# Norm offsets on GpSimd, layer 2's divide on ScalarE, and new booked durations in a planned four-layer graph network

## Chip, cores and metric

The kernel runs on one core of a Trainium2 chip. The metric is the device time in microseconds (us). Engines are named as the profile names them: PE (TensorE, matmul), PEld (its weight loads), DVE (VectorE), ACT (ScalarE), POOL (GpSimd), SP (SyncE, which issues nearly all DMAs).

## The reference

`x` is 32 batches of 512 nodes with 128 features, `adj` a 512x512 weighted adjacency. Four layers follow one another, each as `x = x + layer(relu(layernorm(x)))`:

```
def _layernorm(x, axis=-1, eps=1e-5):
    m = jnp.mean(x, axis=axis, keepdims=True)
    v = jnp.var(x, axis=axis, keepdims=True)
    return (x - m) / jnp.sqrt(v + eps)

# layer 0, GCN:   out = (d (adj+I) d) h W^T + b
# layer 1, GGNN, 5 steps of:
    m_in = adj @ h ; m_out = adj @ h ; av = [m_in, m_out]
    z  = sigmoid(av @ w3.T + u3(h)) ; r = sigmoid(av @ w4.T + u3(h))
    hv = tanh(av @ w5.T + u5(r * h)) ; h = (1 - z) * h + z * hv
# layers 2 and 3, graph attention, h = x W:
    e = leaky_relu(h a_src [i] + h a_dst [j]), masked by adj
    out = softmax(e) @ h          # layer 2: elu(out)
```

All inputs and outputs are fp32.

## The kernel before, in words

A batch is a tile of 128 partitions x 4 chunks x 128 features, 128x512 in the profile. Each batch passes through `gcn` (layer 0, two batches at a time), `ggnn` (layer 1, five calls of `step`) and `gat` twice (layers 2 and 3). Many batches are in flight at once: six "lanes" of layer 1, nine `x` buffers, eight PSUM banks.

**The order of the work.** Nothing is emitted as it is written. Each piece is booked with `op(engine, cost, due, emit, r, w)`: the engine, a cost in us, a due time, a function that issues the instructions, and the values read and written. A `Plan` then simulates all engines with these costs, a delay for the handover from each engine to another (`DELAY`, L64), and the buffers that are free. It tries several ways of setting the priorities (8 rounds for each of two `ends`, each round taking its due times from a pass backwards over the last one), keeps the order with the earliest simulated end, and emits the instructions of every engine's queue in that order. The queues are in order on the chip: an instruction that waits holds up all behind it. So booked costs are not only a description: they decide the order, in all engines' queues and in SP's queue of DMAs. Booked names: `MM` a fp32 matmul of 512 columns, `MR` one in fp32r, `V` a 128x512 operation of DVE, `A` a 128x512 activation, `COPY` a 128x512 copy or scaling by ACT.

**Products in three parts.** A product in layers 0 and 1 (`in_three`, L626) splits its operand into `upper`, `lower` and `across` (`operands`, L612: one ACT instruction, L615, and two of DVE, L616 and L618). PE multiplies `upper` and `lower` (L642), ACT rescales the bank in place (`rescale`, L624), and PE adds `across`. `step` does the same with the gates (L756) and has plain fp32 products (L753). Its gates are ACT's tanh (L786, L793, L797) and DVE's arithmetic (L788, L799, L800, L802).

**The norm.** `norm_relu` (L516) is called by `gcn`, `ggnn` and by `gat` for all but the last four batches: 119 times, and once as `norm_first`. DVE takes statistics of each chunk (L507), aggregates (L511) and adds epsilon (`ve`, L512). POOL raises this to -0.5 (`rstd`, L520). DVE multiplies the mean by -1 and by `rstd` (`off`, L523). ACT applies `relu(rstd * x + off)` in four instructions (L526). For batches 1 to 3 a DVE multiply by `dinv` (L522) follows the power. The last four batches (`near`) use another norm, `center_relu`.

**The turn of tokens to features** is a DVE transpose of 32x32 blocks (`sq`, L592 and L602) and DMAs by way of DRAM, on SP's queue (L595, L597, L605, L608), or PE transposes in the first and last batches.

**Attention.** `gat` (L848): PE makes heads (L869), ACT takes exponents (L885) and scales (L889), a small DMA pair spreads a row over all partitions (L907, L909), DVE makes the weights `e` (L912), and PE mixes (L938) two chunks at a time into a bank, with the softmax's denominator in column `D`. DVE takes its reciprocal `rden` (L941). For layer 2 DVE then divides both chunks in one instruction from the bank, `v = bank * rden` (L943); ACT takes an exponent of `v` (L962), and two DVE instructions (L964, L966) finish the ELU and the residual. Layer 3 divides and adds in one (L948).

Of the kernel before, what the change touches and what calls it, by code (L numbers as in the profile page):

```python
# [10 lines left out]
F32 = mybir.dt.float32  # L11
# [3 lines left out]
ALU = mybir.AluOpType  # L15

P = 128
EPS = 1e-5
# [41 lines left out]
class Plan:  # L60

    DELAY = {"PE": 0.24, "ACT": 0.15, "DVE": 0.12, "POOL": 0.1, "SP": 2.4, "AQ": 2.4}  # L64

    IDLE = 0.11
    SPAN, REST = 3.4, 0.9
# [203 lines left out]
def gnn_stack(ctx: ExitStack, tc: tile.TileContext, a: dict, out: bass.AP):  # L271
    nc = tc.nc
    x, adj = a["x"], a["adj"]
    B, N, D = x.shape
# [46 lines left out]
        IDLE_FROM, lambda v: nc.tensor.transpose(v.t[:, 0, :], ident.t, ident.t))  # L321
    op = plan.op
    MM, MM1, TURN, MR = 0.858, 0.224, 0.111, 0.2325
    V, A, COPY = 0.595, 0.575, 0.495

    def fixed(shape, name, parts=1, dtype=F32):
        v = Val(None, parts)
        v.t = tiles(1, shape, name, dtype=dtype)[0]
        return v
# [13 lines left out]
        return flat(v.t) if len(v.t.shape) == 3 else v.t  # L343

    ident = fixed([P, P], "ident")
    mhalf = fixed(SMALL, "mhalf")
    warm = Val("hv")
    op("POOL", 0.8, -1000, lambda: make_identity(nc, ident.t), w=[ident])
    op("POOL", 0.1, -999, lambda: nc.gpsimd.memset(mhalf.t, -0.5), w=[mhalf])
    op("DVE", 0.1, -1000, lambda: nc.vector.memset(warm.t[:, 0, :], 0.0), w=[warm])  # L350
    op("ACT", 1.4, -1000, lambda: nc.scalar.activation(warm.t[:, 1, :1], warm.t[:, 0, :1], AF.Tanh), r=[warm])

# [149 lines left out]


    def norm_stats(b, due):
        xb, st, mv, ve = xs[b], Val("st", C), Val("mv"), Val("ve")
        for c in range(C):
            op("DVE", 0.192, due, lambda c=c: nc.vector.bn_stats(st.t[:, c, :], xb.t[:, c, :]), r=[xb[c]], w=[st[c]])  # L507

        def aggr():
            for c in range(C):  # L510
                nc.vector.bn_aggr(mv.t[:, c, :], st.t[:, c, :])  # L511
            nc.vector.tensor_scalar_add(ve.t, mv.t[:, :, 1], EPS)  # L512
        op("DVE", 0.33, due, aggr, r=[st], w=[mv, ve])
        return mv, ve

    def norm_relu(b, y, due, times=None):  # L516

        xb, off, rstd = xs[b], Val("off"), Val("rstd")
        mv, ve = norm_stats(b, due)
        op("POOL", 1.0, due, lambda: nc.gpsimd.tensor_tensor(rstd.t, ve.t, mhalf.t, ALU.pow), r=[ve, mhalf], w=[rstd])  # L520
        if times:
            op("DVE", 0.1, due, lambda: nc.vector.tensor_mul(rstd.t, rstd.t, times.t), r=[times], w=[rstd])  # L522
        op("DVE", 0.1, due, lambda: nc.vector.scalar_tensor_tensor(off.t, mv.t[:, :, 0], -1.0, rstd.t, op0=ALU.mult, op1=ALU.mult),  # L523
           r=[mv, rstd], w=[off])
        for c in range(C):
            op("ACT", 0.385, due, lambda c=c: nc.scalar.activation(  # L526
                chunk(y, c), xb.t[:, c, :], AF.Relu, bias=off.t[:, c:c + 1], scale=rstd.t[:, c:c + 1]),
               r=[xb[c], off, rstd], w=[y[c * len(y.writers) // C]])

    def norm_first(b, y):  # L530

        xb, off, f = xs[b], Val("off", C), Val("rstd", C)
        mv, ve = norm_stats(b, -802)
        for parts in ((0, 2, 1), (3,)):
            some = slice(min(parts), max(parts) + 1)
            fs, offs = [f[c] for c in parts], [off[c] for c in parts]

            def power(c=parts[-1], some=some):
                nc.vector.reduce_sum(deg.t[:, c:c + 1], adj_sb.t[:, c, :], axis=mybir.AxisListType.X)
                nc.vector.scalar_tensor_tensor(f.t[:, some], deg.t[:, some], 1.0, ve.t[:, some], op0=ALU.add, op1=ALU.mult)  # L540
            op("DVE", 0.8, -801.5, power, r=[ve, adj_sb[parts[-1]], *(deg[c] for c in parts[:-1])], w=[*fs, deg[parts[-1]]])
            op("POOL", 1.0, -802, lambda some=some: nc.gpsimd.tensor_tensor(
                f.t[:, some], f.t[:, some], mhalf.t[:, some], ALU.pow), r=[mhalf], w=fs)
            op("DVE", 0.1, -801.5, lambda some=some: nc.vector.scalar_tensor_tensor(
                off.t[:, some], mv.t[:, some, 0], -1.0, f.t[:, some], op0=ALU.mult, op1=ALU.mult), r=[mv, *fs], w=offs)
        op("DVE", 0.2, -800.5, lambda: nc.vector.tensor_scalar(
            y.t[:, 0, :], xb.t[:, 0, :], mv.t[:, 0, 0:1], 0.0, op0=ALU.subtract, op1=ALU.max), r=[xb[0], mv], w=[y[0]])
        op("DVE", 0.2, -802, lambda: nc.vector.tensor_scalar_mul(y.t[:, 0, :], y.t[:, 0, :], f.t[:, 0:1]), r=[f[0]], w=[y[0]])
        for c in range(1, C):
            op("ACT", 0.385, -798, lambda c=c: nc.scalar.activation(  # L550
                y.t[:, c, :], xb.t[:, c, :], AF.Relu, bias=off.t[:, c:c + 1], scale=f.t[:, c:c + 1]), r=[xb[c], off[c], f[c]], w=[y[c]])
        op("DVE", 0.1, -801, lambda: nc.vector.tensor_scalar_add(dinv.t, deg.t, 1.0), r=[deg], w=[dinv])
        op("POOL", 1.0, -801, lambda: nc.gpsimd.tensor_tensor(dinv.t, dinv.t, mhalf.t, ALU.pow), r=[mhalf], w=[dinv])
# [34 lines left out]
    def shuttle(src, squares, dst, due, soon):  # L588


        sq, far = Val("sq"), Val("far", Q)
        op("DVE", 0.617, soon, lambda: nc.vector.transpose(  # L592
            sq.t.rearrange("p q (c j) -> p q c j", c=C), flat(src.t).rearrange(squares, c=C, q=Q)), r=[src], w=[sq])
        for k in range(Q):
            op("SP", 0.44, due, lambda k=k: nc.sync.dma_start(  # L595
                far.t[:, :, k, :].rearrange("q i f -> i q f"), sq.t[k * W:(k + 1) * W]), r=[sq], w=[far[k]], delay=4)
        op("SP", 0.4, due, lambda: nc.sync.dma_start(dst.t, far.t.rearrange("q i k f -> (q i) k f")), r=[far], w=[dst], delay=5)  # L597

    def shuttle_first(h, hT, due, soon):

        sq, far = Val("sq"), Val("far", Q)
        op("DVE", 0.617, soon, lambda: nc.vector.transpose(  # L602
            sq.t.rearrange("p k (c i) -> p k c i", c=C), h.t.rearrange("p c (k j) -> p k c j", k=Q)), r=[h], w=[sq])
        for q in range(Q):
            op("SP", 0.44, due, lambda q=q: nc.sync.dma_start(  # L605
                far.t[:, :, q, :].rearrange("k j f -> j k f"), sq.t[q * W:(q + 1) * W]), r=[sq], w=[far[q]], delay=4)
        for q in range(Q):
            op("SP", 0.4, due, lambda q=q: nc.sync.dma_start(  # L608
                hT.t.rearrange("p c (q i) -> q p c i", q=Q)[q], far.t.rearrange("k j q (c i) -> q (k j) c i", c=C)[q]),
               r=[far[q]], w=[hT[q]], delay=5)  # L610

    def operands(src, given, made, due):  # L612

        upper, lower, across = Val("upper"), Val("lower"), Val("across")
        op("ACT", COPY, due - 5, lambda: nc.scalar.mul(made(upper.t), given(src.t), BELOW), r=[src], w=[upper])  # L615
        op("DVE", 0.575, due - 5, lambda: nc.vector.tensor_sub(made(lower.t), given(src.t), made(upper.t).bitcast(F32)),  # L616
           r=[src, upper], w=[lower])
        op("DVE", 0.575, due - 5, lambda: nc.vector.scalar_tensor_tensor(  # L618
            flat(across.t), flat(lower.t).bitcast(F32), -SPLIT, flat(upper.t).bitcast(F32), op0=ALU.mult, op1=ALU.add),
           r=[lower, upper], w=[across])  # L620
        return upper, lower, across
# [226 lines left out]
    def gat(b, l, due):  # L848
# [60 lines left out]
            op("SP", 0.4, due + 1.5, lambda: nc.sync.dma_start(  # L909
                row.t, line.t.rearrange("c q i -> (c q i)").unsqueeze(0).to_broadcast([P, N])), r=[line], w=[row, e], delay=7)  # L910
        for j in range(C):
            op("DVE", 0.65, due + 3, lambda j=j: nc.vector.scalar_tensor_tensor(  # L912
                e.t[:, j, :], matrix(row), h.t[:, j, D + 1:D + 2], mask.t[:, j, :], op0=ALU.max, op1=ALU.mult),
               r=[row, h[2 + j // 2], mask], w=[e[j]])

# [14 lines left out]
        for a, p in enumerate(ps):  # L930
# [8 lines left out]
                                         start=(j == 0), stop=(j == C - 1))  # L939
                op("PE", C * MM1, due + 4, mix, r=[e, h], w=[*ps] if a == c == 0 else [p])  # L940
            op("DVE", 0.08, due + 4, lambda some=some, pt=pt: nc.vector.reciprocal(rden.t[:, some], pt()[:, :per, D]), r=[p], w=[rden[c] for c in chunks])  # L941
            if l == 2:
                op("DVE", 0.335, due + 4, lambda some=some, pt=pt: nc.vector.tensor_mul(  # L943
                    v.t[:, some], pt()[:, :, :D], rden.t[:, some, None].to_broadcast([P, 2, D])), r=[p, rden[2 * a], rden[2 * a + 1]], w=[v[a]])
            else:
                def finish(chunks=chunks, pt=pt):
                    for c, i in enumerate(chunks):
                        nc.vector.scalar_tensor_tensor(xb.t[:, i, :], pt()[:, c, :D], rden.t[:, i:i + 1], xb.t[:, i, :],  # L948
                                                       op0=ALU.mult, op1=ALU.add)
                op("DVE", per * 0.26, due + 4, finish, r=[p, *(rden[c] for c in chunks)], w=[xb[c] for c in chunks])  # L950
# [77 lines left out]
```

## Time and profile before

| what | value |
|---|---|
| median of 3 runs | 1538.93 us (1538.82 to 1539.08) |
| the profiled execution | 1538.23 us, its span 1536.4 us |
| granted TensorE clock | 1.00 |
| busy: PE, PEld | 1514.7 us (99%), 1149.8 (75%) |
| busy: DVE | 1475.1 us (96%), 3725 instructions |
| busy: ACT | 1203.0 us (78%), 2608 instructions |
| busy: POOL | 153.7 us (10%), 137 instructions |
| DMA | 157.76 MB, 103 GB/s, queue share 39.9% of 16 engines |

Busy time is the union of an engine's instructions, as a share of the span from the first instruction to the last. Ends of matmuls are modelled in this profile, so a busy PE need not be PE at its peak. Times inside the span count from its start.

### The profile page before, as it was taken

How to read it: one execution, taken by the hardware profiler on the slowest of the kernel's cores; microseconds unless marked ns; L12 is line 12 of the kernel's file. 1: busy time of each engine (PE TensorE's matmuls, PEld its weight loads, DVE VectorE, ACT ScalarE, POOL GpSimd, SP SyncE). 2: the span in 40 equal slices, each digit the busy share in tenths (PEclk: the TensorE clock that was granted, in tenths of full speed). 3: DMA queues.
4: the chain of work that ended last, by engine and by line, in shares of the span. 5: the costliest groups of instructions: out<-in, count | busy, mean ns of one | idle time of the engine just before them, and what ended most of it. 6: DMA issues, size and time to landing. Idle time of an engine off the chain costs nothing.

```text
span 1536.4 us, 24733 instructions
## 1 busy us (share of the span) xinstructions
PE 1514.7 (99%) x7373; PEld 1149.8 (75%) x7373; DVE 1475.1 (96%) x3725; ACT 1203.0 (78%) x2608; POOL 153.7 (10%) x137
## 2 busy tenths in 40 slices
PE   9999999999999999999999999999999999999998
PEld 7666677777777777777777677777777777777778
DVE  8999989999999999999999999999999999998898
ACT  7877788787978687987788868788887788767664
POOL 2101001010001000101110101100011010001011
PEclk9999999999999999999999999999999999999999
DMA  4233244454544444434444435354443544333111
GB/s 110 42 92 101 75 104 104 102 131 112 131 110 117 115 101 118 121 95 129 114 105 117 111 95 139 96 134 111 114 114 87 130 109 114 96 109 84 42 35 43
DMA packets 270150, 157.76 MB, mean 103 GB/s; under 512 B 81248, under 2 KB 236224, under 8 KB 270016
## 3 DMA queue, kind: packets, MB, share of 16 engines
q1 hardware_dynamic: 269728, 155.66, 39.9%
q8 instruction: 58, 0.95, 0.3%
q14 instruction: 76, 0.62, 0.1%
q10 hardware_dynamic: 288, 0.52, 0.1%
HBM read 86.25 MB, written 69.84 MB: 102 GB/s over the span
## 4 chain that ended last, share of the span: by engine, by line
PE 56%; DVE 29%; ACT 6%; issue 4%; DMA 3%; SPq 1%; POOL 1%; DVEq 0%; POOLq 0%; ACTq 0%
PE bank L642 19%; PE bank L753 13%; PE bank L756 11%; PE bank L938 7%; DVE e L912 4%; DVE lower L616 4%; DVE across L618 3%; DVE sq L592 2%; DVE st L507 2%; PE bank L869 2%; ACT bank L624 2%; DVE hv L799 2%; DVE hT L802 1%; ACT y L526 1%; DVE rh L788 1%
## 5 line engine op out<-in xcount | busy, mean ns | idle before, releaser
L624 ACT ACTIVATE bank<-bank 128x512 f32<-128x512 f32 x748 | 426.3, 593 | 117.1 <-PE bank L642 63.3
L520 POOL TENSOR_TENSOR rstd<-ve,mhalf 128x4 f32<-128x4 f32 x119 | 142.1, 1194 | 1303.2 <-DVE ve L512 868.4
L938 PEld LDWEIGHTS bank<-h_gat,e 128*128 128x128 f32 x1792 | 217.8, 191 | 21.5 <-issue 14.1
L618 DVE SCALAR_TENSOR_TENSOR across<-lower,upper 128x512 fp32r<-128x512 f32 x328 | 221.3, 681 | 2.1 <-PE bank L756 0.4
L938 PE MATMUL bank<-h_gat,e 128*128 128x129 f32 x1792 | 220.3, 275 | 0.1
L756 PE MATMUL bank<-upper,gates 128*128 128x512 f32 x420 | 203.9, 486 | 4.4 <-DVE lower L616 2.0
L756 PE MATMUL bank<-across,gates 128*128 128x512 f32 x420 | 202.3, 491 | 2.6 <-ACT bank L624 2.3
L642 PE MATMUL bank<-adj,across 128*128 128x512 f32 x640 | 189.8, 420 | 0.9 <-ACT bank L624 0.7
L642 PE MATMUL bank<-adj,upper 128*128 128x512 f32 x640 | 189.0, 417 | 0.6 <-ACT h_gat L889 0.4
L642 PE MATMUL bank<-adj,lower 128*128 128x512 f32 x640 | 173.3, 393 | 0.0
L756 PE MATMUL bank<-lower,gates 128*128 128x512 f32 x420 | 166.4, 396 | 0.7 <-DVE lower L616 0.7
L753 PE MATMUL bank<-rh,wT 128*128 128x512 f32 x320 | 164.3, 595 | 2.6 <-DVE rh L788 2.4
L753 PE MATMUL bank<-hT,wT 128*128 128x512 f32 x320 | 163.3, 592 | 0.0
L912 DVE SCALAR_TENSOR_TENSOR e<-row,h_gat,maskT 128x512 f32<-128x512 f32 x224 | 156.4, 745 | 0.0
L642 PEld LDWEIGHTS bank<-adj,upper 128*128 128x128 f32 x640 | 117.9, 188 | 41.7 <-issue 14.1
L642 PEld LDWEIGHTS bank<-adj,across 128*128 128x128 f32 x640 | 117.0, 188 | 42.9 <-issue 13.2
L786 ACT ACTIVATE r<-bank,gate_bw 128x512 f32<-128x512 f32 x160 | 111.1, 694 | 40.4 <-PE bank L753 39.2
L642 PEld LDWEIGHTS bank<-adj,lower 128*128 128x128 f32 x640 | 120.2, 188 | 27.1 <-DVE lower L616 0.2
L793 ACT ACTIVATE z<-bank,gate_bw 128x512 f32<-128x512 f32 x160 | 110.4, 694 | 29.0 <-PE bank L756 22.2
L526 ACT ACTIVATE y<-x,off,rstd 128x128 f32<-128x128 f32 x252 | 111.7, 495 | 19.0 <-DVE off L523 18.9
L797 ACT ACTIVATE hv<-bank,gate_bw 128x512 f32<-128x512 f32 x160 | 111.4, 698 | 12.0 <-PE bank L753 11.8
L799 DVE TENSOR_TENSOR hv<-hv,hT 128x512 f32<-128x512 f32 x160 | 108.7, 680 | 11.6 <-ACT hv L797 11.6
(159 smaller groups left out, 2671.0 us busy)
## 6 DMA issues: line engine op xcount, KB each, us to landing
far<-sq SPq DMA_DIRECT2D x928, 64.0 KB
h<-far SPq DMA_DIRECT2D x148, 256.0 KB
gT<-far SPq DMA_DIRECT2D x56, 256.0 KB
row<-line SPq DMA_DIRECT2D x56, 256.0 KB
hT<-far SPq DMA_DIRECT2D x112, 64.0 KB
x<-in_x_dram SPq DMA_DIRECT2D x24, 256.0 KB
out_dram<-x SPq DMA_DIRECT2D x20, 256.0 KB
adjT<-in_x_dram SPq DMA_DIRECT2D x8, 256.0 KB
```

The lines of the kernel that those rows point to most:

```text
L520: op("POOL", 1.0, due, lambda: nc.gpsimd.tensor_tensor(rstd.t, ve.t, mhalf.t, ALU.pow), r=[ve, mhalf], w=[rstd])
L526: op("ACT", 0.385, due, lambda c=c: nc.scalar.activation(chunk(y, c), xb.t[:, c, :], AF.Relu, bias=off.t[:, c:c + 1], scale=rstd.t[:, c:c ...
L618: op("DVE", 0.575, due - 5, lambda: nc.vector.scalar_tensor_tensor(flat(across.t), flat(lower.t).bitcast(F32), -SPLIT, flat(upper.t).bitca ...
L624: op("ACT", COPY, due, lambda: nc.scalar.mul(flat(p.t), flat(p.t), by), w=[p])
L642: nc.tensor.matmul(flat(p.t), left.t[:, c, :], right.t[:, c, :], start=first and c == 0, stop=c == C - 1, skip_group_check=True)
L753: nc.tensor.matmul(flat(p.t), (of or gates).t[:, i, :], flat(moving.t), start=start, stop=True, skip_group_check=True)
L756: nc.tensor.matmul(flat(p.t), of.t[:, i - 1, :], flat(moving.t), start=start, stop=True, skip_group_check=True)
L786: op("ACT", A, due - 5, lambda: nc.scalar.activation(flat(r.t), flat(gate.t), AF.Tanh, bias=gate_b["w4"].t, scale=0.5), r=[gate, gate_b["w ...
L797: op("ACT", A, due - 5, lambda: nc.scalar.activation(flat(hv.t), flat(cand.t), AF.Tanh, bias=gate_b["w5"].t), r=[cand, z, gate_b["w5"]], w ...
L799: op("DVE", V, due - 5, lambda: nc.vector.tensor_sub(flat(hv.t), flat(hv.t), flat(hT.t)), r=[hT], w=[hv])
L912: op("DVE", 0.65, due + 3, lambda j=j: nc.vector.scalar_tensor_tensor(e.t[:, j, :], matrix(row), h.t[:, j, D + 1:D + 2], mask.t[:, j, :], ...
L938: nc.tensor.matmul(pt()[:, c, :D + 1], e.t[:, j, i * P:(i + 1) * P], h.t[:, j, :D + 1], start=(j == 0), stop=(j == C - 1))
```

## The change

Three things change. In the norm, POOL takes over the addition of epsilon and both multiplications of the offset, in three instructions beside its power; two small DVE instructions go (in `norm_first` the addition stays on DVE). In layer 2 of all but the last four batches, the division of the mix is done by ACT, one instruction for each chunk with `rden` as its column of scales, in place of one DVE instruction for two chunks. And booked costs and delays are changed; these issue nothing, but the planned order follows from them. `...` marks unchanged lines.

```diff
-    DELAY = {"PE": 0.24, "ACT": 0.15, "DVE": 0.12, "POOL": 0.1, "SP": 2.4, "AQ": 2.4}
+    DELAY = {"PE": 0.2, "ACT": 0.15, "DVE": 0.145, "POOL": 0.1, "SP": 2.4, "AQ": 2.4}
...
-    V, A, COPY = 0.595, 0.575, 0.495
+    V, A, COPY = 0.6, 0.575, 0.505
...
-    mhalf = fixed(SMALL, "mhalf")
+    mhalf, eps, minus1 = fixed(SMALL, "mhalf"), fixed(SMALL, "eps"), fixed(SMALL, "minus1")
...
-    op("POOL", 0.1, -999, lambda: nc.gpsimd.memset(mhalf.t, -0.5), w=[mhalf])
+    for v, to in ((mhalf, -0.5), (eps, EPS), (minus1, -1.0)):
+        op("POOL", 0.1, -999, lambda v=v, to=to: nc.gpsimd.memset(v.t, to), w=[v])
...
     def norm_stats(b, due):
-        xb, st, mv, ve = xs[b], Val("st", C), Val("mv"), Val("ve")
+        xb, st, mv = xs[b], Val("st", C), Val("mv")
         for c in range(C):
-            op("DVE", 0.192, due, lambda c=c: nc.vector.bn_stats(st.t[:, c, :], xb.t[:, c, :]), r=[xb[c]], w=[st[c]])
+            op("DVE", 0.196, due, lambda c=c: nc.vector.bn_stats(st.t[:, c, :], xb.t[:, c, :]), r=[xb[c]], w=[st[c]])
 
         def aggr():
             for c in range(C):
                 nc.vector.bn_aggr(mv.t[:, c, :], st.t[:, c, :])
-            nc.vector.tensor_scalar_add(ve.t, mv.t[:, :, 1], EPS)
-        op("DVE", 0.33, due, aggr, r=[st], w=[mv, ve])
-        return mv, ve
+        op("DVE", 0.29, due, aggr, r=[st], w=[mv])
+        return mv
 
     def norm_relu(b, y, due, times=None):
 
         xb, off, rstd = xs[b], Val("off"), Val("rstd")
-        mv, ve = norm_stats(b, due)
-        op("POOL", 1.0, due, lambda: nc.gpsimd.tensor_tensor(rstd.t, ve.t, mhalf.t, ALU.pow), r=[ve, mhalf], w=[rstd])
+        mv = norm_stats(b, due)
+        op("POOL", 1.2, due, lambda: nc.gpsimd.tensor_tensor(rstd.t, mv.t[:, :, 1], eps.t, ALU.add), r=[mv, eps], w=[rstd])
+        op("POOL", 1.2, due, lambda: nc.gpsimd.tensor_tensor(rstd.t, rstd.t, mhalf.t, ALU.pow), r=[mhalf], w=[rstd])
+        op("POOL", 1.2, due, lambda: nc.gpsimd.tensor_tensor(off.t, mv.t[:, :, 0], minus1.t, ALU.mult), r=[mv, minus1], w=[off])
         if times:
             op("DVE", 0.1, due, lambda: nc.vector.tensor_mul(rstd.t, rstd.t, times.t), r=[times], w=[rstd])
-        op("DVE", 0.1, due, lambda: nc.vector.scalar_tensor_tensor(off.t, mv.t[:, :, 0], -1.0, rstd.t, op0=ALU.mult, op1=ALU.mult),
-           r=[mv, rstd], w=[off])
+        op("POOL", 1.2, due, lambda: nc.gpsimd.tensor_tensor(off.t, off.t, rstd.t, ALU.mult), r=[rstd], w=[off])
...
# transposes of shuttle and shuttle_first: 0.617 -> 0.626
# lower and across of operands (L616, L618): 0.575 -> V
# e of gat (L912): 0.65 -> 0.661
...
-            if l == 2:
+            if l == 2 and not near:
+                def divide(chunks=chunks, pt=pt):
+                    for c, i in enumerate(chunks):
+                        nc.scalar.mul(v.t[:, i, :], pt()[:, c, :D], rden.t[:, i:i + 1])
+                op("ACT", 0.52, due + 4, divide, r=[p, *(rden[c] for c in chunks)], w=[v[a]])
+            elif l == 2:
                 op("DVE", 0.335, due + 4, lambda some=some, pt=pt: nc.vector.tensor_mul(
                     v.t[:, some], pt()[:, :, :D], rden.t[:, some, None].to_broadcast([P, 2, D])), r=[p, rden[2 * a], rden[2 * a + 1]], w=[v[a]])
```

More of the change, by code (lines that the diff above doesn't have):

```diff
@@ L532, in norm_first @@
         xb, off, f = xs[b], Val("off", C), Val("rstd", C)
-        mv, ve = norm_stats(b, -802)
+        mv, ve = norm_stats(b, -802), Val("ve")
+        op("DVE", 0.1, -802, lambda: nc.vector.tensor_scalar_add(ve.t, mv.t[:, :, 1], EPS), r=[mv], w=[ve])
         for parts in ((0, 2, 1), (3,)):
@@ L591, in shuttle @@
         sq, far = Val("sq"), Val("far", Q)
-        op("DVE", 0.617, soon, lambda: nc.vector.transpose(
+        op("DVE", 0.626, soon, lambda: nc.vector.transpose(
             sq.t.rearrange("p q (c j) -> p q c j", c=C), flat(src.t).rearrange(squares, c=C, q=Q)), r=[src], w=[sq])
@@ L601, in shuttle_first @@
         sq, far = Val("sq"), Val("far", Q)
-        op("DVE", 0.617, soon, lambda: nc.vector.transpose(
+        op("DVE", 0.626, soon, lambda: nc.vector.transpose(
             sq.t.rearrange("p k (c i) -> p k c i", c=C), h.t.rearrange("p c (k j) -> p k c j", k=Q)), r=[h], w=[sq])
@@ L615, in operands @@
         op("ACT", COPY, due - 5, lambda: nc.scalar.mul(made(upper.t), given(src.t), BELOW), r=[src], w=[upper])
-        op("DVE", 0.575, due - 5, lambda: nc.vector.tensor_sub(made(lower.t), given(src.t), made(upper.t).bitcast(F32)),
+        op("DVE", V, due - 5, lambda: nc.vector.tensor_sub(made(lower.t), given(src.t), made(upper.t).bitcast(F32)),
            r=[src, upper], w=[lower])
-        op("DVE", 0.575, due - 5, lambda: nc.vector.scalar_tensor_tensor(
+        op("DVE", V, due - 5, lambda: nc.vector.scalar_tensor_tensor(
             flat(across.t), flat(lower.t).bitcast(F32), -SPLIT, flat(upper.t).bitcast(F32), op0=ALU.mult, op1=ALU.add),
@@ L911, in gat @@
         for j in range(C):
-            op("DVE", 0.65, due + 3, lambda j=j: nc.vector.scalar_tensor_tensor(
+            op("DVE", 0.661, due + 3, lambda j=j: nc.vector.scalar_tensor_tensor(
                 e.t[:, j, :], matrix(row), h.t[:, j, D + 1:D + 2], mask.t[:, j, :], op0=ALU.max, op1=ALU.mult),
```

## The prediction

> **What bounds the kernel now.** I read the page's busy shares first: PE 99%, DVE 96%, ACT 78%, POOL 10%. Two engines look full, so I asked for the busy time in stretches, then for the groups by form, the waits, and short pieces of the timeline. The stretches (columns: us, then busy us and instructions of PE, PEld, DVE, ACT, POOL):
>
> ```profile
> 160.00:280.00 120.00, 119.90 (x498) 87.14 (x497) 108.85 (x229) 98.77 (x199) 7.72 (x6) 1.00 0.38 96
> 280.00:1320.00 1040.00, 1028.04 (x5023) 787.62 (x5022) 1025.70 (x2526) 837.10 (x1811) 99.83 (x85) 1.00 0.45 114
> 1320.00:1480.00 160.00, 160.00 (x784) 117.45 (x783) 142.34 (x340) 115.36 (x258) 11.84 (x10) 1.00 0.29 77
> ```
>
> In the middle 1040 us, when all four layers are in flight at once, DVE is busy 98.6%; on either side of it 89 to 91%. PE's busy share cannot be compared so directly, because matmul ends are modelled. I therefore count slots, the spacing at which matmuls follow one another when nothing holds them. The longest pieces of the chain give it: L642 x12 in 2.77 us is 0.231 us, L753 x8 in 3.43 is 0.429, L938 x24 in 2.68 is 0.112. With the counts of each stretch PE's slots fill 118.9 of 120 us (99.1%), 1011.7 of 1040 (97.3%) and 159.1 of 160 (99.4%). So where DVE has a tenth of its time free PE is the bound and nearly perfect; where DVE is full, PE loses 28 us. **In the middle DVE is the limit, with PE 28 us behind it.**
>
> The groups that the change touches (busy, mean ns of one | idle before, releaser):
>
> ```profile
> L943 DVE TENSOR_TENSOR v<-bank,rden 128x256 f32<-128x256 f32 x64 | 25.2, 415 | 0.1
> L512 DVE TENSOR_SCALAR ve<-mv 128x4 f32<-128x4 f32 x120 | 20.4, 170 | 4.1
> L523 DVE SCALAR_TENSOR_TENSOR off<-mv,rstd 128x4 f32<-128x4 f32 x119 | 18.2, 154 | 8.3 <-POOL rstd L520 7.2
> L889 ACT ACTIVATE h_gat<-bank,h_gat 128x128 f32<-128x128 f32 x224 | 69.8, 388 | 0.9
> L520 POOL TENSOR_TENSOR rstd<-ve,mhalf 128x4 f32<-128x4 f32 x119 | 142.1, 1194 | 1303.2 <-DVE ve L512 868.4
> ```
>
> A mean is not what an instruction takes of its engine, since the next one starts before it ends. The timeline of DVE shows the slot (start, duration):
>
> ```profile
> 708.57 0.17 DVE L512 TENSOR_SCALAR ve<-mv 128x4 f32<-128x4 f32 x1
> 708.65 0.69 DVE L799 TENSOR_TENSOR hv<-hv,hT 128x512 f32<-128x512 f32 x1
> 709.25 0.68 DVE L788 SCALAR_TENSOR_TENSOR rh<-r,hT 128x512 f32<-128x512 f32 x1
> 709.86 0.68 DVE L800 SCALAR_TENSOR_TENSOR hv<-z,hv 128x512 f32<-128x512 f32 x1
> 710.46 0.15 DVE L523 SCALAR_TENSOR_TENSOR off<-mv,rstd 128x4 f32<-128x4 f32 x1
> 710.53 0.28 DVE L507 BATCH_NORM_STATS2 st<-x 128x6 f32<-128x128 f32 x1
> ```
>
> `ve` takes 0.08 us, `off` 0.07, a 512-wide operation 0.60. Two L943 stand in the timeline as one entry of 0.74 us, and the next instruction starts 0.65 after it: 0.325 each. Last, who waits for whom (total us, times, longest):
>
> ```profile
> PEld bank L756 <- ACT bank L624: 27.6, 63, 1.5
> ACT r L962 <- DVE v L943: 27.3, 19, 3.6
> ACT y L526 <- DVE off L523: 24.6, 35, 2.2
> PEld bank L756 <- DVE lower L616: 10.2, 18, 1.7
> PEld bank L753 <- DVE rh L788: 7.1, 12, 1.1
> ```
>
> PE is held by ACT's rescale of a bank (L624) and by DVE's operands; ACT in turn is held by the two kinds of DVE work that the change takes away.
>
> **The Trainium skill.** "Trainium Kernel Development and Optimization", section Performance Expectations, calls matmul busy time a bad measure of closeness to the roofline; here 99% busy stands against 97.3% of slots. "Perfetto Trace Analysis", section Optimizing Scalar/DVE Operations, says that work may be handed from a saturated DVE to ScalarE or even GpSimd, but that GpSimd and DVE share an SBUF read port. The trace shows DVE undisturbed: L799, L788 and L800 above ran at 0.68 to 0.69 us while L520 ran from 708.88 to 710.20; their groups' means are 0.68. "GPSIMD Engine Reference", section 3.1, has an add of 2048 elements at 4497 ns and about 2.6 cycles an element; at 1.2 GHz that leaves some 60 ns, so an estimate for 128x4 is 0.1 us. No row here shows a plain add or multiply on POOL.
>
> **The change part by part.**
>
> 1. *Norm, DVE side.* `ve` leaves 119 norms (`norm_first` keeps one): 119 x 0.08 = 9.5 us. `off` leaves 119: 119 x 0.07 = 8.3 us, with the 7.2 us that DVE stood waiting for POOL's power. In the middle there are 85 of each: 85 x 0.15 = 12.8 us of slots.
>
> 2. *Norm, POOL side.* One power becomes add, power, multiply by -1, multiply. The power is 1.01 to 1.52 us (1.19 mean). The new ones lie between the estimated 0.1 and the power's 1.5; the order books 1.2 for each. I take 0.5, as a dispatch-dominated guess between both ends. Even at 1.3 a norm is 5.2 us, 119 make 620 us of 1536, so POOL is no bound. Its queue issues no DMA. What changes is latency: from aggregate to ReLU 0.08 + 1.19 + 0.07 and two handovers become 2.5 to 5 us on POOL, without DVE's queue in between. Behind it stand ACT's four L526, then their shuttle on SP or the transpose on PE. The order has six batches in flight, and it places L526 by the booked 4 x 1.2, so short operations only leave slack. Cost taken: nothing while they stay within 1.3; the upper end is rival 3. In batches 1 to 3 a DVE multiply by `dinv` lies in the chain; PE is short of work there (37.57 busy of the first 40 us), so up to 2 us may be lost. I take 1.
>
> 3. *Layer 2's divide.* 56 L943 (8 of 64 belong to the last batches and stay) leave DVE: 56 x 0.325 = 18.2 us, in the middle 46 x 0.325 = 15.0. ACT gains 112 multiplies 128x128 from a bank with a column scale, the same form as L889: 69.8 / 224 = 0.31 each, 35 us, taking ACT from 1203 to 1238 us (81%). The wait of L962 for `v` (27.3 us) becomes a wait of the divide for `rden`, behind the same DVE queue; queued behind it on ACT are rescales that PE needs. ACT is 80% busy in the middle (837 of 1040), so I price this at 4 us of PE time, between 0 and 10.
>
> 4. *Durations.* The order is worked out from booked costs before the kernel starts and then frozen into in-order queues. The old book had L616 and L618 at 0.575 where the timeline shows 0.60: 656 x 0.025 = 16.4 us of DVE work that the old order did not know; some 830 other 512-wide ones at 0.595 (4 us), L912 at 0.65 against 0.661 (2.8), transposes (2). Together 25 us, 1.7% of DVE: the order thinks operands ready before they are, and PE waits on L616 and L788. PE's handover is set from 0.24 to 0.20; at 437.66 the matmul after an L753 starts, and the L797 that waited starts at 437.86, so 0.20 is right. This costs no instruction. But it reshuffles everything, SP's queue of shuttles too; the DMAs stay the same in number, and I price them at nothing, since DMA engines are at 45% and a new order shifts them either way.
>
> *The sum.* DVE in the middle: 12.8 + 15.0 of slots and about 3 of waits, 31 us of 1040, so it could end at 1009. PE stays at 1011.7 of slots, and at the 99.2% of the looser stretches needs 1020: at most 20 us come back. DVE would then still be 98% full, so I take 16, less 4 for ACT. Outside the middle PE is at 99% already; 3 us from better order where DVE holds it in 40 to 160, less 1 in the start. 16 - 4 + 3 - 1 = 14 us. The profiled execution took 1538.23 us (span 1536.4 and 1.8 around it), so 1524; the median of the runs is 0.7 higher: **1525 us**.
>
> **Rivals.** (1) *DVE off the bound altogether*: the order, knowing true costs, keeps PE at 99.2% throughout, and the start and tail gain too: 20 in the middle and 5 to 9 elsewhere, 1511. For it: the flanks do this today. Against: ACT fuller. (2) *Gain eaten by ACT*: PE's largest real wait is already ACT (27.6 against 10.2 and 7.1 for DVE); if the 35 us added there return as PE waits one for two, 17 us go and 1536 to 1538 remains. (3) *POOL's chain late in ACT's queue*: where four POOL instructions take more than the booked 1.2 us with its handover, say 1.5 (the power reached 1.52), each norm's L526 comes 4 x 0.2 = 0.8 us late, 119 x 0.8 = 95 us of ACT waiting at its head, of which a quarter reaches PE by the rescales: 24 us against the 14, so 1549, slower. It decides from about 1.43 us for each POOL instruction. For it: L526 already waits 24.6 us. Against: only the power is known to be long. (4) *The order is just another one*: its parameters (ends, slot, idle point) stay, and an unlucky order costs or gives some 6 us either way; this widens each case.
>
> **How the numbers follow.** What a measurement of this kernel can tell from no change is about 0.2%, 3 us. The forecast has 0.54 (1514 to 1535), rival 1 0.16, rival 2 0.10, rival 3 with unlucky orders 0.20. Faster: the forecast and rival 1, 0.70; same: rival 2 but for 0.02, 0.08; slower: that and rival 3, 0.22. The range 1507 to 1547 leaves out the far ends of rivals 1 and 3.
>
> **What would show it.** Right: DVE's busy time down by about 60 us (20 + 18 + 22 by the groups) and in the middle below 97%; L943 x8; ACT at about 1238; PE's slots above 98% of the middle; waits on L616 and L788 smaller. Wrong in part 2: L526's wait for POOL above 40 us. Wrong in part 3: L756's wait for L624 well above 27.6. The forecast falls if DVE's work drops as said and the span does not.

## The result, and the profile after

The changed kernel takes 1513.94 us (median of 6 runs, 1513.58 to 1515.29) against 1539.16 us before: a ratio of 0.9839, interval 0.9828 to 0.9849, 25 us less. The profiled execution took 1513.58 us, its span 1511.7.

Stretches of the kernel after, with the columns of before (us, then busy us of PE, PEld, DVE, ACT, POOL):

```profile
160.00:280.00 120.00, 120.00 (x517) 88.53 (x516) 108.86 (x229) 101.73 (x211) 17.13 (x28) 1.00 0.38 95
280.00:1320.00 1040.00, 1038.76 (x5116) 809.04 (x5115) 1011.28 (x2344) 887.54 (x1953) 200.82 (x344) 1.00 0.44 115
1320.00:1480.00 160.00, 159.19 (x859) 120.91 (x858) 138.86 (x355) 113.51 (x273) 21.58 (x30) 1.00 0.25 71
```

DVE fills 97.2% of the middle, was 98.6%; ACT went up from 837 to 888 us. PE's slots, counted with the same slot sizes as in the prediction, fill 1035.8 of the 1040 us. I call the rest of a stretch PE's lost time: it fell from 28.3 to 4.2 us in the middle. The chain that ended last says the same. Before, PE had 56% of it and DVE 29%; after:

```profile
PE 95%; DVE 3%; ACT 1%; DMA 1%; issue 0%; ACTq 0%
```

Groups of the changed operations, and of ACT's ReLU, which was L526 and is L527 (busy, mean ns of one | idle before it):

```profile
L520 POOL TENSOR_TENSOR rstd<-mv,eps 128x4 f32<-128x4 f32 x119 | 59.2, 497 | 1110.2 <-DVE mv L512 1049.1 <-DVE rden L943 57.7 <-DVE gate_bw L488 3.2
L521 POOL TENSOR_TENSOR rstd<-rstd,mhalf 128x4 f32<-128x4 f32 x119 | 135.6, 1140 | 0.0
L522 POOL TENSOR_TENSOR off<-mv,minus 128x4 f32<-128x4 f32 x119 | 46.2, 388 | 0.0
L525 POOL TENSOR_TENSOR off<-off,rstd 128x4 f32<-128x4 f32 x119 | 52.1, 439 | 12.0 <-DVE rstd L524 5.2
L950 DVE TENSOR_TENSOR v<-bank,rden 128x256 f32<-128x256 f32 x8 | 3.0, 413 | 0.0
L947 ACT ACTIVATE v<-bank,rden 128x128 f32<-128x128 f32 x112 | 34.6, 367 | 27.2 <-DVE rden L943 26.8
L527 ACT ACTIVATE y<-x,off,rstd 128x128 f32<-128x128 f32 x252 | 113.1, 499 | 0.5 <-POOL off L525 0.4
```

The two small DVE operations are gone, the divide stands on ACT at 0.31 us each, and the last line holds the largest change: ACT's idle time before these ReLUs was 19.0 us and is 0.5. ACT's wait for `v` (27.3 us) did not go; it is a wait for `rden` now (26.8), and 4.4 us are left for the `v` that DVE still makes in the last batches. Of the waits (total us, times, longest) the one of PE that was largest:

```profile
PEld bank L758 <- ACT bank L626: 14.2, 48, 0.7
```

It was 27.6 us. PE's wait for L616 at the same line (10.2) is 0.9, at L618 now.

### The profile page after: what moved, and what is told of

It is laid out like the page before. It is cut to its first block, busy times and chain, and to the rows that moved or that the text cites. A ratio compares the mean times of both kernels' runs of the same rounds, so it can differ in the third digit from the quotient of the medians.

```text
span 1511.7 us, 24916 instructions
## 1 busy us (share of the span) xinstructions
PE 1498.9 (99%) x7366; PEld 1153.8 (76%) x7366; DVE 1430.9 (95%) x3431; ACT 1236.2 (82%) x2720; POOL 292.9 (19%) x496
## 4 chain that ended last, share of the span: by engine, by line
PE 95%; DVE 3%; ACT 1%; DMA 1%; issue 0%; ACTq 0%
PE bank L644 34%; PE bank L755 21%; PE bank L758 19%; PE bank L940 13%; PE bank L871 4%; PE bank L717 2%; PE bank L926 1%; PE bank L586 1%; DVE e L914 1%; DMA rh<-in_L_gnn_w_w_dram 0%; DMA e<-in_adj_dram 0%; PE bank L667 0%; DVE x L721 0%; DVE st L563 0%; DVE e L685 0%
## 5 line engine op out<-in xcount | busy, mean ns | idle before, releaser
L520 POOL TENSOR_TENSOR rstd<-mv,eps 128x4 f32<-128x4 f32 x119 | 59.2, 497 | 1110.2 <-DVE mv L512 1049.1
L758 PE MATMUL bank<-across,gates 128*128 128x512 f32 x420 | 198.8, 487 | 0.2 <-ACT bank L626 0.2
L521 POOL TENSOR_TENSOR rstd<-rstd,mhalf 128x4 f32<-128x4 f32 x119 | 135.6, 1140 | 0.0
L795 ACT ACTIVATE z<-bank,gate_bw 128x512 f32<-128x512 f32 x160 | 110.4, 692 | 18.1 <-PE bank L758 15.4
L799 ACT ACTIVATE hv<-bank,gate_bw 128x512 f32<-128x512 f32 x160 | 111.2, 696 | 11.9 <-PE bank L755 11.7
```

The source lines that it names most:

```text
L521: op("POOL", 1.2, due, lambda: nc.gpsimd.tensor_tensor(rstd.t, rstd.t, mhalf.t, ALU.pow), r=[mhalf], w=[rstd])
L758: nc.tensor.matmul(flat(p.t), of.t[:, i - 1, :], flat(moving.t), start=start, stop=True, skip_group_check=True)
L795: op("ACT", A, due - 5, lambda: nc.scalar.activation(flat(z.t), flat(gate.t), AF.Tanh, bias=gate_b["w3"].t, scale=0.5), r=[gate, gate_b["w ...
L799: op("ACT", A, due - 5, lambda: nc.scalar.activation(flat(hv.t), flat(cand.t), AF.Tanh, bias=gate_b["w5"].t), r=[cand, z, gate_b["w5"]], w ...
```

## The experiments

PE's lost time by stretch ties every run to its place. Span less lost time is 1489 to 1494 us in all of them, 1490.1 before and 1489.3 after, so this table accounts for the spans to within 4 us. Each kernel ran beside runs of before on its own chip, whose medians were 1538.6 to 1539.2 us. "Median" is of all runs of a kernel, in us; the lost times are those of its one profiled execution, which lies within 2.2 us of that median.

| kernel | median | lost 0-40 | 40-280 | 280-1320 | later |
|---|---|---|---|---|---|
| before | 1538.9 | 5.7 | 5.3 | 28.3 | 7.0 |
| e_operands | 1534.6 | 6.1 | 2.1 | 23.3 | 9.9 |
| e_durations | 1529.8 | 5.4 | 1.5 | 23.2 | 7.6 |
| e_slack | 1530.4 | 10.5 | 3.1 | 17.7 | 6.5 |
| e_ve | 1526.8 | 6.6 | 1.2 | 16.6 | 8.6 |
| e_off | 1525.9 | 4.7 | 1.1 | 19.4 | 6.9 |
| e_work | 1522.9 | 11.5 | 1.9 | 10.9 | 7.3 |
| e_divide_dur | 1522.6 | 5.3 | 1.0 | 17.3 | 7.5 |
| e_norm_dur | 1516.7 | 11.4 | 1.7 | 5.1 | 7.0 |
| the change | 1513.9 | 9.8 | 1.3 | 4.2 | 7.1 |
| e_start | 1517.0 | 6.8 | 3.7 | 5.3 | 7.9 |
| e_pool_book | 1531.2 | 5.3 | 2.5 | 18.1 | 9.7 |
| e_pool_08 | 1511.6 | 4.7 | 1.2 | 7.5 | 6.3 |
| e_after_slot | 1515.5 | 11.9 | 0.8 | 4.7 | 7.1 |

**The three parts.** My first two theories were "relief" (DVE was full, and only taking work from it helps) and "book" (the old order was frozen on wrong costs). `e_durations` has the new booked numbers alone; it is the change with the divide and the norm's two operations back on DVE:

```diff
-            if l == 2 and not near:
+            if False:
...
+            nc.vector.tensor_scalar_add(ve.t, mv.t[:, :, 1], EPS)
-        op("DVE", 0.29, due, aggr, r=[st], w=[mv])
+        op("DVE", 0.37, due, aggr, r=[st], w=[mv, ve])
...
+        op("POOL", 1.2, due, lambda: nc.gpsimd.tensor_tensor(rstd.t, ve.t, mhalf.t, ALU.pow), r=[ve, mhalf], w=[rstd])
...
+        op("DVE", 0.1, due, lambda: nc.vector.scalar_tensor_tensor(off.t, mv.t[:, :, 0], -1.0, rstd.t, op0=ALU.mult, op1=ALU.mult),
+           r=[mv, rstd], w=[off])
```

> Booked durations and delays of the change alone; norm and divide stay as before (the norm's aggregate with its addition is booked at 0.37, the power at 1.2). Theory 'relief' (DVE was full in the middle, and only taking work from it helps): DVE stays at about 98.5% of 280 to 1320 us, PE's slots gain little there, time 1530 to 1539 us. Theory 'book' (the order was frozen on too low DVE costs, and PE waited for operands that it was told would be ready): waits of PE on L616 and L788 shrink, and the time is 1520 to 1527 us with the same DVE work.

Measured 1529.80 us, ratio 0.9943 (0.9928 to 0.9958). `e_work` is the other half: the moved work of the change, with `DELAY`, `V`, `COPY`, L616, L618, the transposes, `e` and the statistics booked as before.

> Both moves of work (norm offsets to POOL, divide to ACT) with all booked durations and delays of before, but for the moved instructions themselves. 'Relief': most of the gain is here, 1515 to 1522 us. 'Book': the order still books 656 operand instructions at 0.575 and PE still waits, 1527 to 1535 us. If each alone brings more than half, they overlap: both only lift PE to its limit.

Measured 1522.88 us, ratio 0.9892 (0.9875 to 0.9908). So the numbers bring 9.1 us without the work (PE's waits for `lower` and `rh` are 3.3 and 2.9 us, were 10.2 and 7.1, as "book" said), and the work brings 16.1 without the numbers. Neither theory has it alone. That the two sum to the change's 25 may be luck, since every kernel has another order. And `e_work` keeps the 1.2 us at which the change books each of POOL's instructions, so its 16.1 us are those of the move together with that booking. `e_norm_dur` has `if False:` for the divide only; `e_divide_dur` has only the norm put back.

> The change without the divide on ACT: DVE keeps 56 L943 of 0.325 us, 18 us of slots. 'Relief': in proportion to DVE's slots, half of the gain from work is lost, 1520 to 1526 us. 'Book': PE is at its limit nearly as well, 1514 to 1519 us. If the 35 us on ACT cost PE 4 us as I priced, this kernel wins them back.

> The change without the norm on POOL: DVE keeps ve and off, 18 us of slots and its waits for POOL's power. 'Relief': 1520 to 1526 us, and DVE waits for POOL some 7 us again. 'Book': 1514 to 1519 us. At the start, where PE lost 4 us of slots in the first 40 us of the changed kernel, batches 1 to 3 have one POOL instruction again in place of four: if that chain was the cause, the first 40 us come back to about 34 us of slots.

Measured 1516.74 us (ratio 0.9856, 0.9842 to 0.9871) and 1522.64 us (0.9894, 0.9879 to 0.9908). On top of the new numbers the norm is worth 13.1 us alone and the divide 7.2 alone, though both take 18 us of slots from DVE; on top of the norm, the divide adds 2.8. The middle stretch, first of `e_durations`, then of `e_norm_dur`, then of `e_divide_dur`:

```profile
280.00:1320.00 1040.00, 1029.80 (x5018) 789.94 (x5017) 1024.50 (x2542) 848.07 (x1829) 102.97 (x87) 1.00 0.44 114
```

```profile
280.00:1320.00 1040.00, 1039.43 (x5096) 805.42 (x5095) 1024.29 (x2385) 865.80 (x1869) 209.72 (x346) 1.00 0.45 115
```

```profile
280.00:1320.00 1040.00, 1033.89 (x5054) 797.53 (x5053) 1017.84 (x2509) 876.09 (x1934) 105.59 (x87) 1.00 0.44 114
```

With the norm moved, DVE is as full as without (1024 us) and yet PE loses only 5.1 us in place of 23.2. So DVE's busy share does not tell what PE loses. It does not acquit DVE, though: over the whole span DVE is busy 1469.4 us in `e_durations` and 1449.1 in `e_norm_dur`, and a DVE that is equally full in both gets through more of the program in the same 1040 us. By the prediction's count the move frees 12.8 us of its slots in the middle, where PE gains 18.1. ACT's queue differs too, first `e_durations`, then `e_norm_dur`:

```profile
L527 ACT ACTIVATE y<-x,off,rstd 128x128 f32<-128x128 f32 x252 | 112.7, 494 | 20.6 <-DVE off L524 20.4
```

```profile
L527 ACT ACTIVATE y<-x,off,rstd 128x128 f32<-128x128 f32 x252 | 110.7, 495 | 0.7 <-POOL off L525 0.7
```

ACT stood 20.6 us at the head of its queue for an offset that stood in DVE's full queue; PE's rescales are behind it in the same queue. What this costs PE can be traced. I followed each wait of PE for a rescale back along ACT's queue to ACT's last pause, taking a pause from 0.15 or from 0.30 us on and going back 14 or 40 instructions at most. In before, 19 to 25 of the 42 us of such waits lead back to an ACT that stood for `off`; in `e_durations` 4 to 10 of 44; in `e_norm_dur` none of 22. In `e_durations` the head of the queue is thus a part of the 18 us, and DVE's freed slots can be the larger one.

**Which half of the norm?** `e_off` leaves only the offsets on POOL, `e_ve` only the addition of epsilon; both without the divide. First `e_off`, then `e_ve`, each against `e_norm_dur`:

```diff
-        op("POOL", 1.2, due, lambda: nc.gpsimd.tensor_tensor(rstd.t, mv.t[:, :, 1], eps.t, ALU.add), r=[mv, eps], w=[rstd])
+            nc.vector.tensor_scalar_add(ve.t, mv.t[:, :, 1], EPS)
...
```

```diff
-        op("POOL", 1.2, due, lambda: nc.gpsimd.tensor_tensor(off.t, mv.t[:, :, 0], minus1.t, ALU.mult), r=[mv, minus1], w=[off])
...
-        op("POOL", 1.2, due, lambda: nc.gpsimd.tensor_tensor(off.t, off.t, rstd.t, ALU.mult), r=[rstd], w=[off])
+        op("DVE", 0.1, due, lambda: nc.vector.scalar_tensor_tensor(off.t, mv.t[:, :, 0], -1.0, rstd.t, op0=ALU.mult, op1=ALU.mult),
+           r=[mv, rstd], w=[off])
```

> As the kernel with the norm on POOL and the new durations but no divide on ACT (1516.7 us), with epsilon's addition back on DVE (0.08 us of DVE in 119 norms); only the offsets are on POOL. Theory 'slots': the norm's part of the gain (1529.8 to 1516.7) follows DVE's slots, so half of it comes back: about 1523 us. Theory 'head of the queue': it is ACT, which waited 23 us at L527 for an offset that stood in DVE's full queue, with PE's rescales behind it; that wait stays away here, so 1516 to 1519 us.

> The mirror of the last: addition of epsilon on POOL, the offset back on DVE (0.07 us in 119 norms), new durations, no divide on ACT. 'Slots': about 1523 us. 'Head of the queue': ACT waits for DVE's offset again, some 20 us in all, and the time is 1526 to 1530 us.

Measured 1525.91 and 1526.77 us (ratios 0.9918, 0.9903 to 0.9933; 0.9925, 0.9910 to 0.9940). "Head of the queue" falls as I had put it: `e_off` has ACT's wait down to 2.7 us and yet brings only 3.9 of the 13.1. "Slots" expected half, 1523, and falls short too. Each half brings 3 to 4 us, both 13. In the middle alone, PE's lost time falls by 3.8 us in `e_off`, 6.6 in `e_ve` and 18.1 with both, for some 6, 7 and 13 us of freed slots: there "slots" does better than in the medians, but the two halves together still bring more than their slots.

**Is it the work, or the booking?** The norm's path is booked at 4 x 1.2 us and four handovers of 0.1, 5.2 us; `e_pool_book` books the shortest times that the trace of after shows, 0.2 for the add and both multiplies (their lines are changed in the same way) and 1.0 for the power, with nothing else touched. The means in the groups above are longer, 0.39 to 0.50 and 1.14.

```diff
-        op("POOL", 1.2, due, lambda: nc.gpsimd.tensor_tensor(rstd.t, mv.t[:, :, 1], eps.t, ALU.add), r=[mv, eps], w=[rstd])
-        op("POOL", 1.2, due, lambda: nc.gpsimd.tensor_tensor(rstd.t, rstd.t, mhalf.t, ALU.pow), r=[mhalf], w=[rstd])
+        op("POOL", 0.2, due, lambda: nc.gpsimd.tensor_tensor(rstd.t, mv.t[:, :, 1], eps.t, ALU.add), r=[mv, eps], w=[rstd])
+        op("POOL", 1.0, due, lambda: nc.gpsimd.tensor_tensor(rstd.t, rstd.t, mhalf.t, ALU.pow), r=[mhalf], w=[rstd])
```

> The change, with POOL's four instructions booked as the trace has them: 0.2, 1.0, 0.2, 0.2 in place of 1.2 each. If latency of the norm costs, or the start was spoilt by the long booking, it gains: 1508 to 1512 us, the start back to 34 us of slots. If the long booking is slack that lets every offset be ready before ACT reaches it, ACT's wait at L527 returns (over 10 us) and the time is 1516 to 1522 us.

Measured 1531.22 us, ratio 0.9955 (0.9938 to 0.9972): the same instructions on the same engines, 17 us slower for shorter booked numbers, and 9 us beyond the slower of the two ranges that I had given. It is also 8.6 us slower than `e_divide_dur`, which leaves the norm on DVE: moved with this booking, the norm costs time. Its middle stretch and its waits:

```profile
280.00:1320.00 1040.00, 1032.53 (x5046) 795.59 (x5045) 996.25 (x2309) 872.62 (x1930) 196.46 (x338) 1.00 0.45 114
```

```profile
ACT y L527 <- POOL off L525: 35.0, 30, 4.2
PEld bank L758 <- ACT bank L626: 25.9, 70, 3.1
```

DVE has more free time than in the change (95.8% against 97.2%), and PE loses 18.1 us, because ACT now waits at its head for POOL's offset and PE's wait for the rescale is 25.9 us again, from 14.2. Of PE's 41 us of waits for rescales, 22 to 26 lead back to an ACT that stood for `off`; in the change it is at most 0.2 of 19. Here the head of the queue is shown without DVE in the play. The cause of the lateness stands in POOL's timeline of the changed kernel, two norms (start, us):

```profile
305.50 0.20 POOL L520 TENSOR_TENSOR rstd<-mv,eps 128x4 f32<-128x4 f32 x1 [21.04 <-DVE rden L943]
305.65 0.20 POOL L522 TENSOR_TENSOR off<-mv,minus 128x4 f32<-128x4 f32 x1
305.80 1.01 POOL L521 TENSOR_TENSOR rstd<-rstd,mhalf 128x4 f32<-128x4 f32 x1
306.88 0.41 POOL L525 TENSOR_TENSOR off<-off,rstd 128x4 f32<-128x4 f32 x1
...
327.97 0.56 POOL L520 TENSOR_TENSOR rstd<-mv,eps 128x4 f32<-128x4 f32 x1 [16.05 <-DVE mv L512]
328.48 0.65 POOL L522 TENSOR_TENSOR off<-mv,minus 128x4 f32<-128x4 f32 x1
329.09 1.46 POOL L521 TENSOR_TENSOR rstd<-rstd,mhalf 128x4 f32<-128x4 f32 x1
330.62 0.32 POOL L525 TENSOR_TENSOR off<-off,rstd 128x4 f32<-128x4 f32 x1
```

One chain ends 1.8 us after its start, the other 3.0. Over the 74 norms whose four instructions stand together the median is 2.45 us and one in twenty is over 3.9. A plan that books 1.6 and four handovers, 2.0 us, is late in 48 of these 74 norms; one that books 5.2 in none, as the longest takes 5.0.

**Slack without the move.** If slack is all, one number in `e_durations` should do it:

```diff
-        op("POOL", 1.2, due, lambda: nc.gpsimd.tensor_tensor(rstd.t, ve.t, mhalf.t, ALU.pow), r=[ve, mhalf], w=[rstd])
+        op("POOL", 4.8, due, lambda: nc.gpsimd.tensor_tensor(rstd.t, ve.t, mhalf.t, ALU.pow), r=[ve, mhalf], w=[rstd])
```

> The kernel with the new durations alone (1529.8 us), with one number changed: POOL's power in the norm is booked at 4.8 us in place of 1.2. No instruction is added, removed or moved to another engine; the norm's two small operations stay on DVE. Theory 'slack' (the norm on POOL gains because its four bookings of 1.2 keep ACT's ReLU from being placed before its offset is there, where it would hold the rescales behind it): ACT's wait for the offset falls from 23 us to under 8, and the time is 1516 to 1521 us. Theory 'work' (what counts is that DVE is rid of the two operations and of its turn after POOL): 1528 to 1534 us, as long latency only takes buffers.

Measured 1530.40 us, ratio 0.9943 (0.9926 to 0.9959), no gain over `e_durations`. Its ReLU group:

```profile
L527 ACT ACTIVATE y<-x,off,rstd 128x128 f32<-128x128 f32 x252 | 112.1, 495 | 9.6 <-DVE off L524 9.2
```

With the other ReLU groups ACT waits 17 us for the offset, was 23, and not under 8 as "slack" had it. DVE is busy 99% of the middle (the third busy time below), and PE's largest wait for rescales rose from 28.1 us to 34.3:

```profile
280.00:1320.00 1040.00, 1034.43 (x5068) 796.98 (x5067) 1029.92 (x2554) 849.76 (x1831) 105.84 (x87) 1.00 0.45 115
PEld bank L757 <- ACT bank L625: 34.3, 84, 2.2
```

My reading, which no run tests by itself, is that the longer booking cannot do on DVE what it does on POOL: POOL is idle four fifths of the time in the change and starts a norm when its statistics are there, while an offset on DVE stands in a full in-order queue and comes when that queue comes to it. In the middle PE's lost time falls by 5.5 us, and 5.1 are lost in the first 40. So a longer booking does not bring the gain without the move, and the move does not bring it without the longer booking.

**Between the two bookings.** `e_pool_08` books 0.8 for each of POOL's four.

> The change with POOL's four instructions booked at 0.8 each, 3.6 us with handovers, between the 2.0 of the last kernel (1531 us) and the 5.2 of the change (1514 us). The chain took 1.6 to 3.9 us in the changed kernel's trace, median 2.45. 'Slack': ACT's wait at L527 is under 8 us and the time near the change's, 1512 to 1518 us. If the gain grew evenly with the booking it would be 1522 to 1525 us.

Measured 1511.61 us, ratio 0.9822 (0.9807 to 0.9836). ACT waits 3.7 us in its ReLU groups, under the 8 that "slack" had said, so the gain does not grow evenly with the booking: 3.6 us for the norm is enough. The kernel stands 2.3 us below the change, but the intervals overlap. What the trace does show is where the two differ: the first 40 us lose 4.7 us here and 9.8 in the change, the middle 7.5 and 4.2.

**The start.** The change loses 4.1 us more in the first 40 us than before. `e_start` gives batches 1 to 3 the old norm:

```diff
+        if times:
+            op("DVE", 0.1, due, lambda: nc.vector.tensor_scalar_add(rstd.t, mv.t[:, :, 1], EPS), r=[mv], w=[rstd])
+            op("POOL", 1.2, due, lambda: nc.gpsimd.tensor_tensor(rstd.t, rstd.t, mhalf.t, ALU.pow), r=[mhalf], w=[rstd])
+        else:
...
```

> The change, but batches 1 to 3 keep the old norm (addition and offset on DVE). If POOL's chain of four with a DVE multiply in its middle is what took 4 us of PE's slots in the first 40 us, they come back: 1509 to 1511 us, slots of the first 40 us about 34. If the start is set by something else (a later landing of the weights, another order), 1513 to 1515 us.

Measured 1517.04 us, ratio 0.9859 (0.9844 to 0.9874): the first 40 us get 3.0 back, the next stretches lose 2.4, and the whole is not better (neither of my ranges holds). The table settles the cause better than this run: `e_pool_book` and `e_pool_08` issue the change's POOL instructions at the start and lose 5.3 and 4.7 us there, as before does; the kernels that book 4.8 us for the norm lose 9.8 to 11.5, `e_slack` with its one POOL instruction among them. Two of these, `e_work` and `e_norm_dur`, had a lower granted clock in the profiled start (0.58 and 0.66 from 10 to 15 us), which adds to their loss; the change and `e_slack`, at 1.00 throughout, lose 9.8 and 10.5. So the start goes with the booked length, not with the chain.

**How much is chance?** I meant a change of `SLOT` to give another order of the same work.

> The change with SLOT (the factor by which a backward pass is turned into due times) at 9.6 in place of 9.7: another order of the same work with the same booked costs. It shows how much two orders differ by chance. I expect within 3 us of the change, 1511 to 1517 us; if it is off by 6 or more, differences of 3 to 4 us between my kernels say nothing of their edits.

```diff
-    SLOT = 9.7
+    SLOT = 9.6
```

It came out with the very order of the change on every engine, so it is a repeat of it: 1515.53 us, ratio 0.9846 (0.9831 to 0.9860). It says that a repeat lies within 1.6 us, and nothing on chance in orders. What sets the repeat apart is the clock at the start: its trace has a granted clock of 0.66 from 10 to 15 us where the change's has 1.00, and loses 11.9 us of the first 40 in place of 9.8. Of the ten runs of this one order, the five with a mean clock of 1.000 took 1513.6 to 1514.0 us, the five at 0.998 or 0.999 took 1514.3 to 1515.9. I therefore draw nothing from differences of 3 us between kernels with different orders. Larger ones have some support: four different orders with the whole norm on POOL, booked at 0.8 or 1.2 an instruction and with the new numbers (the change, `e_norm_dur`, `e_start`, `e_pool_08`), lose 4.2 to 7.5 us in the middle, and the six that have some of it on DVE or the short booking lose 16.6 to 23.2.

**What was wrong in the old book?** `e_operands` is the kernel before with the two costs of `operands` corrected:

```diff
-        op("DVE", 0.575, due - 5, lambda: nc.vector.tensor_sub(made(lower.t), given(src.t), made(upper.t).bitcast(F32)),
+        op("DVE", 0.6, due - 5, lambda: nc.vector.tensor_sub(made(lower.t), given(src.t), made(upper.t).bitcast(F32)),
...
-        op("DVE", 0.575, due - 5, lambda: nc.vector.scalar_tensor_tensor(
+        op("DVE", 0.6, due - 5, lambda: nc.vector.scalar_tensor_tensor(
```

> The kernel before with L616 and L618 booked at 0.600 in place of 0.575, nothing else. 'Book' as I wrote it down (these 16 us of unknown DVE work were most of what was wrong with the old order): most of the 9 us of the new durations, 1530 to 1533 us. If handovers or the other durations count for more: 1535 to 1539 us.

Measured 1534.61 us, ratio 0.9971 (0.9960 to 0.9982): 4.0 us, under half of the 9.1. What the handovers and the smaller corrections bring each was not split.

## Why the prediction came out as it did

The forecast was 1525 us with a gain of 14; measured was 1513.9 us, a gain of 25 and 1.8 times the forecast. Direction and place were right: PE's loss in the middle came back. Its size was too small, as two things that carried it, the long booking and the new numbers, had no price there. The middle's 24.1 us stand against 12 (16 less 4), the start's loss of 4.1 against 1. That the result lies inside the range owes something to a range 40 us wide.

*The bound.* Right in size: PE lost 28.3 us in the middle, and 24.1 came back. "In the middle DVE is the limit" was a part of it: 19 to 25 us of PE's waits in before lead back to an ACT that stood for `off`. The looser stretches served as the measure of what PE can reach, 99.2%; it reached 99.6%.

*The middle, "16, less 4 for ACT".* The mis-sized term. PE's lost time fell by 24.1 us. I stopped at 16 because DVE would still be 98% full; `e_norm_dur` has DVE at 98.5% and PE loses 5.1 us. How full an engine is did not say how much gets through it, nor how late it is for others. The prediction shows ACT's 24.6 us of waiting for `off` at L526, but no term of its sum prices what PE gets back when that wait goes.

*The divide, "4 us of PE time, between 0 and 10".* No such cost appeared. The divide gained 7.2 us without the norm and 2.8 with it (too little to tell from another order), and PE's wait for ACT's rescale fell to 14.2 us though ACT was fuller. Its `rden` wait, named as the danger, did come, 26.8 us.

*POOL's latency, "nothing while they stay within 1.3".* Right in the numbers: the plain operations have means of 0.39 to 0.50 us where I took 0.5, and the power 1.14. The shortest plain one took 0.19 us, where the prediction's estimate was 0.1. What I passed over in a half-sentence, that "short operations only leave slack", is 17 us: `e_pool_book`.

*Rival 3, ACT late for POOL.* It did not come about in the change (0.4 us of waiting) and it does in `e_pool_book`, by the mechanism described, 37 us of ACT waiting in its ReLU groups. My point of decision, 1.43 us an instruction (1.42 by its own figures), was stated against the booking of 1.2 and is one of the booking, not of POOL alone. *Rival 2* is refuted by the fall of PE's wait for ACT. *Rival 1*, 1511 us, described the outcome best from 40 us on, with PE's slots at 99% and more of the stretches up to 1480 us; its gain at the start and the tail did not come (9.8 us lost in the first 40, was 5.7; 7.1 after 1320, was 7.0).

*The durations.* They brought 9.1 us alone. The forecast had no term for them apart from 3 us in the early stretch; of that stretch 40 to 280, the loss fell from 5.3 to 1.3 us. The 16.4 us of L616 and L618 that I had called the most of it are 4.0 by `e_operands`.

*The start, "less 1".* It was 4.1, and by the table it goes with the booked length and not with the multiply by `dinv` in the chain.

*What would show it.* "DVE's busy time down by about 60 us" was a slip: it fell by 44 (1475.1 to 1430.9). The group sums include tails under which the next instruction already runs; the slots that I had counted two paragraphs earlier are 36. ACT at 1236 us and L943's 8 instructions came as said.

**Left open.** The norm's 13 us are not split further. DVE's freed slots alone are not enough (`e_pool_book`), nor is a longer booking alone (`e_slack`), nor either half of the norm (`e_off`, `e_ve`). How much of the 13 comes from room on DVE and how much from ACT no longer standing for the offset is not shown: in `e_durations` the second accounts for 4 to 10 us of PE's waits. How much is an order that happened to be good is not known either, since no second order of the same booking was run.

## What to carry to other kernels

In a kernel with frozen in-order queues, look for small operations whose reader stands at the head of another engine's queue: the offsets took 8.3 us of DVE's slots in before, but ACT stood 29 us for them, and 19 to 25 us of PE's waits lead back to that. Move such an operation to an engine that is mostly idle, and book its path from the slow end of what it takes: here 3.6 and 5.2 us did for a chain with a median of 2.45, and 2.0, from the shortest times, lost more than the move had brought. A booking of the mean was not run. After a change, count PE's slots by stretch, and tell apart the moved work from the new numbers by a run of each.

## What the hardware showed that I had not expected

POOL's instructions of 128x4 have two paces. In the timeline above the multiply by -1 is followed by the power after 0.15 us or after 0.61. What DVE was doing then, first at the fast norm, then at the slow one:

```profile
305.46 0.67 DVE L618 TENSOR_TENSOR lower<-bank,upper 128x512 fp32r<-128x512 f32 x1
306.05 0.60 DVE L955 SCALAR_TENSOR_TENSOR x<-bank,rden,x 128x128 f32<-128x128 f32 x2
...
328.39 0.68 DVE L971 SCALAR_TENSOR_TENSOR v<-v,x 128x512 f32<-128x512 f32 x1
329.00 0.68 DVE L618 TENSOR_TENSOR lower<-h,upper 128x512 fp32r<-128x512 f32 x1
```

At the slow norm DVE reads two tensors from SBUF, at the fast one an input is a bank. Of the 91 places in the trace where the power follows that multiply, 26 have a gap over 0.3 us, and at all 26 DVE is in a TENSOR_TENSOR or SCALAR_TENSOR_TENSOR without a bank as input when the multiply starts; 21 others beside such an operation are fast, 20 of them beside one with a bank among its inputs, and beside transposes, statistics or an idle DVE none is slow. "GPSIMD Engine Reference" of the Trainium skill, section 8, names contention on shared SBUF interfaces with DVE instructions of two SBUF inputs. The trace agrees, with some 0.45 us for an instruction that meets one, and DVE's own operations did not lengthen (`lower`, L616 before and L618 after, has a mean of 0.68 us in both kernels). That is one reason why a booking from POOL's best times is late.
